# A graph layer on one core: edge groups of 2048 with per-partition sums by node, in place of groups of 1024 with one-hot products for every edge

## Chip, core and metric

The kernel runs on one core of a Trainium2 chip, in one launch. The metric is the device time of that core in microseconds (us), the median of three runs. A further execution was recorded by the hardware profiler; every duration below comes from that one recording.

## What is computed

The reference is one layer of a graph network on 6250 nodes with 64 features and 206250 edges, all fp32. The edges are sorted by their target `dst` before the kernel gets them; each node also has an edge to itself.

```python
h   = max(layernorm(x), 0)                      # 6250 x 64
msg = relu(h[src] + edge_attr)                  # 206250 x 64
agg = segment_sum(msg, dst, 6250)               # sum of the messages of each target node
out = x + relu((h + agg) @ W1 + b1) @ W2 + b2
```

A node has 33 edges on average (206250/6250), so 1024 edges in a row touch about 31 nodes and 2048 about 62.

## The kernel before, in words

**Groups.** The edges are taken in groups of `GE = P * G = 128 * 8 = 1024` in their sorted order. Partition p of group g holds the eight edges that follow each other from `g * 1024 + 8 * p`. There are `NG = 201` full groups and a tail group of four columns (`CT`), which makes `201 * 8 + 4 = 1612` columns of 128 edges.

**Loads.** For each group `load` (called from `window_sum`) gets a tile `ea` (the edge features, one 256 KB transfer on SyncE's queue, L121) and a tile `xg` (the rows `h[src]`). `xg` is filled by `gather` (L128 to L130): one indirect DMA for each column, issued by GpSimd (POOL), each with 128 row numbers that it finds in the SBUF tile `src_sb`. Both tiles come from a pool of `LOOK = 12` buffers, so that POOL and SyncE can be up to twelve groups ahead of VectorE. The first `RAW = 4` groups gather rows of the input `x` and normalise them edge by edge (`norm_edges`), since the normalised rows `h_rows` are not yet in DRAM then.

**Start.** Layer norm of all nodes (`ln_head`, `ln_rows`), the write of `h_rows`, and the transpose into `z`, a tile of 64 x 6250 that holds h (later h + agg) with features on partitions (`ln_turn`). `slot` (L219) is each edge's node number less that of the first node of its group, plus 1.

**The loop over groups, `window_sum`.** VectorE compares `slot` with the numbers 1 to 64 and gets a one-hot tile `oh` in bf16 (L294; `wslots` lies in PSUM). It adds `xg` and `ea`, both in SBUF, into `full`, a tile in PSUM (L299). ScalarE and VectorE then take turns to split relu(full) into three bf16 parts whose sum is the fp32 value (L301, L302, L304, L305). TensorE multiplies: eight products with the one-hot of a column as weights and the 192 part values as the moving operand add up in `agg`, 64 nodes x 3 x 64 (L308). One group later VectorE sums the three parts (`turn`, L278), TensorE transposes (L280), and one more group later VectorE adds the result to 64 columns of `z` that start at a register's value (`sum_into_z`, L285).

**Blocks.** When all edges of a block of 512 nodes are summed (`READY`), `hidden` and `result` do the two dense layers of it and store 128 KB through SyncE's queue (L330). The block's output tile waits for VectorE (L328), and later `ea` loads stand behind that store in the same queue.

**Order.** The order on each engine is the order of the program text: `window_sum(g)`, `turn(g-1)`, `sum_into_z(g-2)`, `blocks_behind(g-2)`. A check (`find_left`) sets a flag if an edge fell outside its window of 64 nodes or came after its block was finished; then a slow path at the end runs all edges again. It is not taken with these inputs.

Of the kernel before, what the change touches and what calls it, by code (L numbers as in the profile page):

```python
# [18 lines left out]
P = 128  # L19
G = 8  # L20
# [3 lines left out]
TP, TG = 71, 6  # L24
assert TP * TG == TE
TJ = 3
# [3 lines left out]
W = 64  # L30
WB = 512
R = 4
# [4 lines left out]
LOOK = 12  # L37
LAG = 2
RV = 8
RAW = 4  # L40
READY = [min(NG, -(-E * P * R * (c + 1) // (N * GE)) + 1) for c in range(NB)]
# [4 lines left out]
def kernel(  # L46
# [20 lines left out]
    work = ctx.enter_context(tc.tile_pool(name="work", bufs=4))  # L67
# [78 lines left out]
    def norm_edges(xg):  # L146
        s = lnp.tile([P, XC * R], F32, name="ln_s")
# [3 lines left out]
        sq = lnp.tile([P, XC * R, D], F32, name="ln_sq")  # L151
        nc.scalar.activation(sq[:, :G], xg, AF.Square)
        v = lnp.tile([P, XC * R], F32, name="ln_v")
# [6 lines left out]
    def ln_head(c):  # L160
        xv, p, n = ((x_sb[:, c:c + XC].rearrange("p b r d -> p (b r) d"), P, XC * R) if c < NB
                    else (x_sb[:TN, NB, 0:1, :], TN, 1))
        s = lnp.tile([P, XC * R], F32, name="ln_s")
# [4 lines left out]
        sq = lnp.tile([P, XC * R, D], F32, name="ln_sq")  # L168
# [3 lines left out]
    def ln_rows(c, xc, sq, p, n):  # L172
        v = lnp.tile([P, XC * R], F32, name="ln_v")
# [16 lines left out]
    def ln_turn(c, h):  # L190
        for b in range(XC if c < NB else 1):
            pt = psum.tile([D, R, P], F32, name="big", bufs=1)
            n0 = (c + b) * P * R
            if c < NB:
                for r in range(R):
                    nc.tensor.transpose(pt[:, r, :], h[:, b * R + r, :], ident)  # L196
                nc.scalar.copy(z[:, n0:n0 + P * R].rearrange("d (p r) -> d r p", r=R), pt)  # L197
            else:
                nc.tensor.transpose(pt[:, 0, :TN], h[:TN, 0, :], ident[:TN, :TN])
                nc.scalar.copy(z[:, n0:N], pt[:, 0, :TN])  # L200

    heads, rows = [], []
# [6 lines left out]
    rows.append(ln_rows(*heads[-1]))  # L209
    ln_turn(*rows[-2])  # L210
# [3 lines left out]
    base = const.tile([1, NG + 1], F32, name="base")  # L214
    nc.vector.tensor_copy(base, dst_sb[0:1, 0:C + 1:G])
    pb = psum.tile([P, R * D], F32, name="out", bufs=1)
    nc.tensor.matmul(pb[:, :NG + 1], ones[0:1, :], base, start=True, stop=True)
# [10 lines left out]

    def combine(xg, ea, n):
# [7 lines left out]
    flag = const.tile([1, 1], I32, name="flag")  # L237

    def find_left():
        nc.vector.tensor_scalar(left, slot, 1.0, None, op0=ALU.is_lt)  # L240
        nc.vector.scalar_tensor_tensor(left, slot, float(W), left, op0=ALU.is_gt, op1=ALU.add)
# [5 lines left out]
        nc.tensor.matmul(pf[0:1, 0:1], most, ones[:, 0:1], start=True, stop=True)  # L247

# [23 lines left out]

    turned = {}

    def turn(g):
        pa = aggs.pop(g)
        rows = work.tile([W, D], F32, name="agg_rows")
        nc.vector.tensor_reduce(rows, pa.rearrange("w t d -> w d t"), AX.X, ALU.add)  # L278
        pt = psum.tile([D, W], F32, name="turned", bufs=1)
        nc.tensor.transpose(pt, rows, ident[:W, :W])  # L280
        turned[g] = pt

    def sum_into_z(g):
        at = window_start(g)
        nc.vector.tensor_tensor(z[:, ds(at, W)], z[:, ds(at, W)], turned.pop(g), ALU.add)  # L285

    def window_sum(g):
        n = G if g < NG else CT
        cols = cols_of(g)
        ea, xg = loaded[g] if g < RAW else load(g)  # L290
        if g < RAW:
            norm_edges(xg)
        oh = work.tile([P, G, W], BF16, name="oh")
        nc.vector.tensor_tensor(  # L294
            oh[:, :n], slot[:, cols].unsqueeze(2).to_broadcast([P, n, W]),
            wslots.unsqueeze(1).to_broadcast([P, n, W]), ALU.is_equal)

        full = psum.tile([P, G, D], F32, name="full", bufs=2)
        nc.vector.tensor_tensor(full[:, :n], xg[:, :n], ea[:, :n], ALU.add)  # L299
        parts = work.tile([P, G, 3, D], BF16, name="parts")  # L300
        nc.scalar.activation(parts[:, :n, 0, :], full[:, :n], AF.Relu)  # L301
        nc.vector.scalar_tensor_tensor(full[:, :n], full[:, :n], 0.0, parts[:, :n, 0, :],  # L302
                                       op0=ALU.max, op1=ALU.subtract)
        nc.scalar.copy(parts[:, :n, 1, :], full[:, :n])  # L304
        nc.vector.tensor_tensor(parts[:, :n, 2, :], full[:, :n], parts[:, :n, 1, :], ALU.subtract)  # L305
        pa = psum.tile([W, 3, D], F32, name="agg", bufs=2)
        for j in range(n):
            nc.tensor.matmul(pa, oh[:, j, :], parts[:, j], start=(j == 0), stop=(j == n - 1))  # L308
# [3 lines left out]
    def hidden(c):  # L312
        n0 = c * P * R
        p, r = (P, R) if c < NB else (TN, 1)
        p1 = psum.tile([D, P * R], F32, name="big", bufs=1)
# [5 lines left out]
    def result(c, h1):  # L321
# [3 lines left out]
        for k in range(r):  # L325
            nc.tensor.matmul(p2[:p, k * D:(k + 1) * D], h1[:, k, :p], w2_sb, start=True, stop=True)  # L326
        o = work.tile([P, R, D], F32, name="o")
# [5 lines left out]
    hid = {}  # L333

    def blocks_behind(g):
        for c in sorted(hid):
            result(c, hid.pop(c))
# [4 lines left out]
    for g in range(NG + 1):  # L342
        window_sum(g)
        if g >= 1:
            turn(g - 1)
        if g >= LAG:
            sum_into_z(g - LAG)
            blocks_behind(g - LAG)
        if g == 8:
            find_left()  # L350
# [5 lines left out]
    sum_into_z(NG + 1 - LAG)  # L356
    blocks_behind(NG + 1 - LAG)
    turn(NG)
    for g in range(NG + 2 - LAG, NG + 1):
        sum_into_z(g)  # L360
        blocks_behind(g)
    hid[NB] = hidden(NB)
    for c in sorted(hid):
        result(c, hid.pop(c))


    def all_windows(msg, lf, n):
        for w in range(0, N, WB):
# [3 lines left out]
            pw = psum.tile([D, WB], F32, name="big", bufs=1)  # L372
# [7 lines left out]
    with tc.If(any_left > 0):  # L380
# [17 lines left out]
        for c in range(NB + 1):  # L398
            result(c, hidden(c))
# [39 lines left out]
```

## Time and profile before

| quantity | value |
|---|---|
| median of three runs | 2051.29 us (2049.82 to 2052.92) |
| the profiled execution's own time | 2389.6 us |
| its span, first to last instruction | 2387.8 us |
| POOL busy in the span | 1584.1 us (66%) |
| VectorE (DVE) busy | 668.4 us (28%) |
| TensorE busy (PE) | 414.4 us (17%) |
| ScalarE (ACT) busy | 267.7 us (11%) |
| mean DMA rate | 47 GB/s |
| start of the first gather, start of the last | 5.7 us, 2335.4 us |

A row of the page's list of groups names the line, the engine, the operation, what it writes and reads with shapes, the count, then busy time in us, the mean of one in ns, and after the second bar the idle time of that engine ahead of it with what ended most of it. The list of waits gives who waited for whom, the sum in us, how often, and the longest. A row of the timeline gives start and duration in us; the bracket is the idle time before it. A gather's row (DMA_INDIRECT on POOL) is the time in which POOL prepares the transfer, not that in which the rows arrive.

### The profile page before, as it was taken

What the parts mean: (1) busy time and instruction counts of PE and PEld (TensorE: products, weight loads), DVE (VectorE), ACT (ScalarE), POOL (GpSimd) and SP (SyncE); (2) the same over time, 40 slices, a digit from 0 to 9 for tenths busy, and PEclk for the clock granted to TensorE, in tenths of its full rate; (3) what the DMA queues carried; (4) which work ended last, traced back from release to release, by engine and by line L of the source; (5) the groups of instructions that cost most, each with busy time, mean ns of one, the idle gap of its engine ahead of it and who ended that gap; (6) DMA issues with size and microseconds to landing.
All of it is one profiled execution on the core that took longest, in us unless ns stands there. A gap on an engine that the chain in (4) does not pass through costs nothing.

```text
span 2387.8 us, 9645 instructions
## 1 busy us (share of the span) xinstructions
PE 414.4 (17%) x1991; PEld 287.2 (12%) x1991; DVE 668.4 (28%) x1321; ACT 267.7 (11%) x450; POOL 1584.1 (66%) x1619
## 2 busy tenths in 40 slices
PE   2000201102102202131112111111202122201123
PEld 1000201101101101020101111011201011101112
DVE  3312612213312413150213223123313123312235
ACT  3100101001100101020101101001101011101012
POOL 6775775766667666677576676575766756775751
DMA  4111112113111312211311311121311131310120
GB/s 156 39 39 31 27 26 91 26 23 89 32 22 25 94 23 48 69 28 26 92 26 22 93 30 21 49 71 20 93 31 22 27 92 22 94 35 19 26 85 8
DMA packets 87526, 112.95 MB, mean 47 GB/s; under 512 B 30949, under 2 KB 35685, under 8 KB 87461
## 3 DMA queue, kind: packets, MB, share of 16 engines
q0 software_dynamic: 51584, 52.93, 11.4%
q1 hardware_dynamic: 34628, 57.65, 7.2%
q10 hardware_dynamic: 1248, 1.70, 0.2%
q14 instruction: 49, 0.39, 0.1%
q8 instruction: 17, 0.28, 0.0%
HBM read 108.96 MB, written 3.20 MB: 47 GB/s over the span
## 4 chain that ended last, share of the span: by engine, by line
another core or an unknown queue 35%; issue 27%; POOL 16%; DVE 11%; ACT 4%; DMA 3%; DVEq 2%; PE 1%; SPq 0%; ACTq 0%; POOLq 0%
POOL xg L130 16%; DVE full L299 3%; DVE full L302 3%; DMA xg<-h_rows,src_sb 2%; ACT parts L301 2%; DVE parts L305 2%; ACT parts L304 2%; DVE oh L294 1%; DVEq L265 1%; DVE agg_rows L278 1%; DMA ea<-in_edge_attr_dram 1%; DVEq L299 1%; PE agg L308 0%; DVE z L285 0%
## 5 line engine op out<-in xcount | busy, mean ns | idle before, releaser
L130 POOL DMA_INDIRECT xg<-h_rows,src_sb x1580 | 1550.1, 981 | 738.3 <-issue 454.5
L308 PE MATMUL agg<-parts,oh 128*64 128x192 bf16 x1612 | 299.8, 367 | 935.5 <-issue 548.2
L308 PEld LDWEIGHTS <-oh 128*64 128x64 bf16 x1612 | 229.9, 168 | 989.9 <-issue 571.6
L278 DVE TENSOR_REDUCE agg_rows<-agg 64x64 f32<-64x192 f32 x202 | 69.4, 344 | 839.4 <-remote 714.3
L301 ACT ACTIVATE parts<-full 128x512 bf16<-128x512 f32 x202 | 120.2, 595 | 1610.2 <-DVE full L299 1184.5
L280 PE MATMUL turned<-ident,agg_rows 64*64 64x64 f32 x202 | 63.1, 312 | 978.7 <-issue 603.4
L302 DVE SCALAR_TENSOR_TENSOR full<-full,parts 128x512 f32<-128x512 f32 x202 | 141.1, 698 | 289.7 <-issue 135.5
L305 DVE TENSOR_TENSOR parts<-full,parts 128x512 bf16<-128x512 f32 x202 | 139.4, 690 | 131.3 <-ACT parts L304 77.9
L299 DVE TENSOR_TENSOR full<-xg,ea 128x512 f32<-128x512 f32 x202 | 138.4, 685 | 46.8 <-DMA ea<-in_edge_attr_dram 26.2
L280 PEld LDWEIGHTS turned<-ident,agg_rows 64*64 64x64 f32 x202 | 25.5, 126 | 1041.1 <-issue 651.1
L294 DVE TENSOR_TENSOR oh<-slot,wslots 128x512 bf16<-128x512 f32 x202 | 135.7, 672 | 0.0
L304 ACT CAST parts<-full 128x512 bf16<-128x512 f32 x202 | 118.0, 584 | 154.4 <-DVE full L302 110.7
L285 DVE TENSOR_TENSOR z<-z,turned 64x64 f32 x202 | 42.1, 208 | 233.7 <-issue 126.0
L130 POOL DMA_INDIRECT xg<-in_x_dram,src_sb x32 | 32.8, 1024 | 13.3 <-issue 9.4
L328 DVE TENSOR_TENSOR o<-out,x_sb 128x256 f32<-128x256 f32 (+1 forms) x13 | 5.3, 409 | 118.5 <-remote 103.7
L318 ACT ACTIVATE h<-big,b_sb 64x512 f32<-64x512 f32 (+1 forms) x13 | 8.5, 656 | 266.4 <-remote 176.8
L316 PE MATMUL big<-z,w_sb 64*64 64x512 f32 (+1 forms) x26 | 24.2, 1032 | 0.3 <-DVE z L285 0.3
L326 PE MATMUL out<-w_sb,h 64*128 64x64 f32 (+1 forms) x98 | 23.6, 418 | 1.2 <-ACT h L318 1.2
L326 PEld LDWEIGHTS out<-w_sb,h 64*128 64x128 f32 (+1 forms) x98 | 22.3, 329 | 3.2 <-ACT h L318 3.2
L196 PE MATMUL big<-ident,ln_h 128*64 128x128 f32 x48 | 12.7, 421 | 45.2 <-DVE ln_h L178 19.1
L197 ACT COPY z<-big 64x512 f32<-64x512 f32 x12 | 12.6, 1051 | 23.2 <-remote 14.4
L196 PEld LDWEIGHTS big<-ident,ln_h 128*64 128x64 f32 x48 | 6.5, 159 | 51.0 <-issue 38.9
(52 smaller groups left out, 63.7 us busy)
## 6 DMA issues: line engine op xcount, KB each, us to landing
ea<-in_edge_attr_dram SPq DMA_DIRECT2D x201, 256.0 KB
xg<-h_rows,src_sb POOLq DMA_INDIRECT x1580
x_sb<-in_x_dram SPq DMA_DIRECT2D x4, 384.0 KB
h_rows<-ln_h SPq DMA_DIRECT2D x4, 384.0 KB
out_dram<-o SPq DMA_DIRECT2D x12, 128.0 KB
dst_sb<-in_dst_main_dram ACTq DMA_DIRECT2D x1, 804.0 KB
src_sb<-in_src_main_dram ACTq DMA_DIRECT2D x1, 788.0 KB
xg<-in_x_dram,src_sb POOLq DMA_INDIRECT x32
```

The costliest lines, as they stand in the source:

```text
L130: nc.gpsimd.indirect_dma_start(out=xg[:, j, :], out_offset=None, in_=rows[:, :], in_offset=bass.IndirectOffsetOnAxis(ap=idx[:, j:j + 1], a ...
L278: nc.vector.tensor_reduce(rows, pa.rearrange("w t d -> w d t"), AX.X, ALU.add)
L280: nc.tensor.transpose(pt, rows, ident[:W, :W])
L285: nc.vector.tensor_tensor(z[:, ds(at, W)], z[:, ds(at, W)], turned.pop(g), ALU.add)
L294: nc.vector.tensor_tensor(oh[:, :n], slot[:, cols].unsqueeze(2).to_broadcast([P, n, W]), wslots.unsqueeze(1).to_broadcast([P, n, W]), ALU. ...
L299: nc.vector.tensor_tensor(full[:, :n], xg[:, :n], ea[:, :n], ALU.add)
L301: nc.scalar.activation(parts[:, :n, 0, :], full[:, :n], AF.Relu)
L302: nc.vector.scalar_tensor_tensor(full[:, :n], full[:, :n], 0.0, parts[:, :n, 0, :], op0=ALU.max, op1=ALU.subtract)
L304: nc.scalar.copy(parts[:, :n, 1, :], full[:, :n])
L305: nc.vector.tensor_tensor(parts[:, :n, 2, :], full[:, :n], parts[:, :n, 1, :], ALU.subtract)
L308: nc.tensor.matmul(pa, oh[:, j, :], parts[:, j], start=(j == 0), stop=(j == n - 1))
L326: nc.tensor.matmul(p2[:p, k * D:(k + 1) * D], h1[:, k, :p], w2_sb, start=True, stop=True)
```

## The change

- Groups have 2048 edges: `G = 16`, so each partition holds 16 edges that follow each other. There are 100 full groups and a tail of 12 columns; the number of columns is `100 * 16 + 12 = 1612`. `LOOK` is 7 groups, `RAW` is 3, `LAG` is 4, the window has 96 nodes.
- Once at the start, `cut` makes three masks over all edges on VectorE: `first` (the edge's node is that of the partition's first edge in the group), `last` (that of its last edge, unless it is the same node), and `mid` (one node between them). `run_slot` holds the three nodes' slots for each group and partition.
- In the loop the sum `xg + ea` is written back into `xg` in SBUF. For each of the three masks VectorE makes `msg = max(xg, 0) * mask` and reduces it over the partition's 16 edges into 64 values. ScalarE's splitting into bf16 parts is gone.
- TensorE gets three fp32 products for a group, with the 64 sums as weights and a one-hot of 96 columns as the moving operand. The product comes out with features on partitions, so the sum of parts, the transpose and `turn` are gone. `one_hot` runs once for two groups.
- `result` is split: the store comes at least one group later (`store`). `READY` is worked out with a margin of 1500 edges. `find_left` asks for edges that none of the three masks covers too. PSUM buffers are dealt out anew; `base` is spread earlier.

The diff, cut to its core:

```diff
-G = 8
+G = 16
+RUNS = 3
...
-W = 64
+W = 96
...
-LOOK = 12
-LAG = 2
+LOOK = 7
+LAG = 4
+OB = 2
 RV = 8
-RAW = 4
-READY = [min(NG, -(-E * P * R * (c + 1) // (N * GE)) + 1) for c in range(NB)]
+RAW = 3
+LW = max(XC * R, G)
+SPARE = 1500
+READY = [min(NG, (E * P * R * (c + 1) // N + SPARE) // GE) for c in range(NB)]
...
+    of_run = [const.tile([P, C + CT], F32, name=f"run{k}") for k in range(RUNS)]
+    run_slot = const.tile([P, NG + 1, RUNS + 1], F32, name="run_slot")
+
+    def cut(g, n, cols, k):
+
+        sv = slot[:, cols].rearrange("p (g j) -> p g j", j=k)
+        first, last, mid = [t[:, cols].rearrange("p (g j) -> p g j", j=k) for t in of_run]
+        nc.vector.tensor_tensor(first, sv, sv[:, :, 0:1].to_broadcast([P, n, k]), ALU.is_equal)
+        nc.vector.tensor_tensor(last, sv, sv[:, :, k - 1:k].to_broadcast([P, n, k]), ALU.is_equal)
+        nc.vector.tensor_tensor(last, last, first, ALU.is_gt)
+        nc.vector.tensor_copy(run_slot[:, g:g + n, 0], sv[:, :, 0])
+        nc.vector.tensor_copy(run_slot[:, g:g + n, 1], sv[:, :, k - 1])
+        nc.vector.tensor_tensor(mid, first, last, ALU.add)
+        nc.vector.scalar_tensor_tensor(mid, mid, 0.5, sv, op0=ALU.is_lt, op1=ALU.mult)
+        nc.vector.tensor_reduce(run_slot[:, g:g + n, 2], mid, AX.X, ALU.max)
+        nc.vector.tensor_tensor(mid, mid, run_slot[:, g:g + n, 2:3].to_broadcast([P, n, k]), ALU.is_equal)
+
+    cut(0, NG, slice(0, C), G)
...
+    def one_hot(g, n, runs):
+        oh = work.tile([P, OB, RUNS + 1, W], F32, name="oh", bufs=3)
+        nc.vector.tensor_tensor(
+            oh[:, :n, :runs], run_slot[:, g:g + n, :runs].unsqueeze(3).to_broadcast([P, n, runs, W]),
+            wslots.unsqueeze(1).unsqueeze(1).to_broadcast([P, n, runs, W]), ALU.is_equal)
...
     def window_sum(g):
-        n = G if g < NG else CT
-        cols = cols_of(g)
+        n, runs = (G, RUNS) if g < NG else (TJ, RUNS + 1)
+        if g % OB == 0 and g < NG:
+            one_hot(g, min(OB, NG - g), RUNS)
+        elif g == NG:
+            one_hot(g, 1, RUNS + 1)
+        oh = hots.pop(g)
         ea, xg = loaded[g] if g < RAW else load(g)
         if g < RAW:
             norm_edges(xg)
-        oh = work.tile([P, G, W], BF16, name="oh")
-        nc.vector.tensor_tensor(
-            oh[:, :n], slot[:, cols].unsqueeze(2).to_broadcast([P, n, W]),
-            wslots.unsqueeze(1).to_broadcast([P, n, W]), ALU.is_equal)
-
-        full = psum.tile([P, G, D], F32, name="full", bufs=2)
-        nc.vector.tensor_tensor(full[:, :n], xg[:, :n], ea[:, :n], ALU.add)
-        parts = work.tile([P, G, 3, D], BF16, name="parts")
-        nc.scalar.activation(parts[:, :n, 0, :], full[:, :n], AF.Relu)
-        nc.vector.scalar_tensor_tensor(full[:, :n], full[:, :n], 0.0, parts[:, :n, 0, :],
-                                       op0=ALU.max, op1=ALU.subtract)
-        nc.scalar.copy(parts[:, :n, 1, :], full[:, :n])
-        nc.vector.tensor_tensor(parts[:, :n, 2, :], full[:, :n], parts[:, :n, 1, :], ALU.subtract)
-        pa = psum.tile([W, 3, D], F32, name="agg", bufs=2)
-        for j in range(n):
-            nc.tensor.matmul(pa, oh[:, j, :], parts[:, j], start=(j == 0), stop=(j == n - 1))
+
+        sums = work.tile([P, RUNS + 1, D], F32, name="sums", bufs=LAG + 2)
+        m = n if g < NG else CT
+        nc.vector.tensor_tensor(xg[:, :m], xg[:, :m], ea[:, :m], ALU.add)
+        for k in range(RUNS):
+            msg = work.tile([P, G, D], F32, name="msg")
+            col = cols_of(g).start
+            nc.vector.scalar_tensor_tensor(
+                msg[:, :n], xg[:, :n], 0.0, of_run[k][:, col:col + n].unsqueeze(2).to_broadcast([P, n, D]),
+                op0=ALU.max, op1=ALU.mult)
+            nc.vector.tensor_reduce(sums[:, k], msg[:, :n].rearrange("p j d -> p d j"), AX.X, ALU.add)
+        if g == NG:
+            nc.vector.tensor_scalar(sums[:, RUNS], xg[:, TJ], 0.0, None, op0=ALU.max)
+        if g % OB == 0:
+            banks.append(psum.tile([D, OB, W], F32, name="agg", bufs=3))
+        pa = banks[-1][:, g % OB]
+        for k in range(runs):
+            nc.tensor.matmul(pa, sums[:, k], oh[:, k], start=(k == 0), stop=(k == runs - 1))
         aggs[g] = pa
...
     for g in range(NG + 1):
         window_sum(g)
-        if g >= 1:
-            turn(g - 1)
         if g >= LAG:
             sum_into_z(g - LAG)
             blocks_behind(g - LAG)
+        if g == 5:
+            find_left()
         if g == 8:
-            find_left()
+            judge()
```

## The prediction

> **What bounds the kernel now.** I read the page's busy times and list of groups, then the list of waits, then the timeline inside the loop, then its last microseconds. From the list of groups:
>
> ```profile
> L130 POOL DMA_INDIRECT xg<-h_rows,src_sb x1580 | 1550.1, 981 | 738.3 <-issue 454.5
> L299 DVE TENSOR_TENSOR full<-xg,ea 128x512 f32<-128x512 f32 x202 | 138.4, 685 | 46.8 <-DMA ea<-in_edge_attr_dram 26.2
> L278 DVE TENSOR_REDUCE agg_rows<-agg 64x64 f32<-64x192 f32 x202 | 69.4, 344 | 839.4 <-remote 714.3
> ```
>
> POOL's gathers are the only work near the length of the run. In a quiet stretch of the timeline a gather is busy for 0.944 us and the next follows 0.305 us later, a pitch of 1.249 us; 1612 of them make 2013 us of a span of 2387.8. The mean is 981 ns, not 944: summed over all gathers, records longer than 0.944 us add 63 us. The rest of the idle time is this, from the list of waits:
>
> ```profile
> POOL xg L130 <- DVE full L299: 262.1, 31, 16.8
> DVE agg_rows L278 <- remote: 714.3, 62, 17.5
> ```
>
> 31 times POOL was twelve groups ahead and waited for L299 to free a buffer, about 254 us beyond the usual gap. VectorE was late because it waited at L278 for TensorE, for up to 17.5 us, though TensorE's products are recorded as done long before. These waits lie 0.70 us apart (14.70, 15.39, 16.09, 16.79, 17.49), and in bursts VectorE takes a group every 4.4 us. So the profiled execution is gathers (5.7 us to the first, 2013) + lengthening 63 + waits 254 + a tail of 52 after the last gather = 2388. Without the waits, and with a tail of 18 (last gather's landing 2.2 us, then the 16 us that the last group takes from its L299 at 2371.8), it would be 2100. The median of the runs is 2051, below even that: unprofiled, POOL is not held up by TensorE at all, and its pitch, lengthening included, is at most (2051 - 6 - 18 - 2)/1612 = 1.256 us. I take the runs as bound by POOL from end to end.
>
> Where the 63 us come from is seen in the timeline of a burst:
>
> ```profile
> 1169.89 0.68 DVE L299 TENSOR_TENSOR full<-xg,ea 128x512 f32<-128x512 f32 x1
> 1170.22 1.16 POOL L130 DMA_INDIRECT xg<-h_rows,src_sb  x1 [0.30 <-issue]
> 1171.30 0.70 DVE L302 SCALAR_TENSOR_TENSOR full<-full,parts 128x512 f32<-128x512 f32 x1 [0.72 <-issue]
> 1171.69 0.94 POOL L130 DMA_INDIRECT xg<-h_rows,src_sb  x1 [0.30 <-issue]
> 1172.65 0.69 DVE L305 TENSOR_TENSOR parts<-full,parts 128x512 bf16<-128x512 f32 x1 [0.65 <-ACT parts L304]
> 1172.94 0.94 POOL L130 DMA_INDIRECT xg<-h_rows,src_sb  x1 [0.30 <-issue]
> 1174.18 1.56 POOL L130 DMA_INDIRECT xg<-h_rows,src_sb  x1 [0.30 <-issue]
> 1174.25 0.69 DVE L299 TENSOR_TENSOR full<-xg,ea 128x512 f32<-128x512 f32 x1
> ```
>
> A gather that starts during L299 is long; one that starts during L302 or L305 is not. L299 reads two SBUF tiles, L302 and L305 one of SBUF and one of PSUM. Over all gathers the rule is tight: one that starts between 0.085 us before and (duration - 0.126) us after the start of a VectorE operation with two SBUF inputs is lengthened until that operation's end less 0.126 us; others are not. L299 accounts for 52 of the 63 us. L150, L167 (tensor_tensor with a broadcast operand), L157, L178 (scalar_tensor_tensor with one) and L241 hold gathers in the same way (1.32 us at L241); the reductions L148, L154, L164, L174, L278 and L294 (one input in PSUM) do not.
>
> **What the Trainium skill says.** "SBUF — State Buffer", section "SBUF: two separate sides", says VectorE and GpSimd share a pair of SBUF ports under an exclusive lock; a VectorE operation with two SBUF inputs holds it for its whole length against a GpSimd operation that reads SBUF. The trace agrees, as above. "Vector Engine (DVE) Microarchitecture Reference", section "Measured stream behaviour on trn2", says a read keeps the full rate only while elements come in adjacent pairs, and prices a source that hops at every element at 1.73 ns a column, against 1.05. No VectorE row of this trace shows that for SBUF plainly; ScalarE's L197, which writes with a 16-byte step, takes 1051 ns for 512 columns where L301 takes 595. "Perfetto Trace Analysis", section "DMA Instruction — SWDGE (GPSIMD)", says the record ends when the descriptors are made, not at the data; here rows land 2.13 us (median) after a record of 0.944 us starts.
>
> **The change, part by part.**
> *Gathers.* 1612 before, 100 x 16 + 12 = 1612 after: nothing.
> *Removed off the path.* L301 and L304 (ACT, 238 us), L302, L305, L278 and 202 one-hots (DVE, 486 us), 1612 bf16 products and the transposes (PE): no gather waits for them in the runs, so zero. If TensorE's lag were real in the runs, see the first rival. Fp32 products, 3 a group with features out, lie in 20 us of gathers: zero.
> *VectorE's length.* L299 takes 418 ns for 256 columns and 686 for 512: 150 ns + 1.047 a column, so 1.22 us for 1024. A group then costs add 1.22 + three multiplies 3.67 + three reductions + half a one-hot 0.4 + z 0.25. A reduction reads with a step of 64 words: at full rate (L164, 947 ns for 768) 1.22 us, with the page's 1.73 ns 1.92 us (estimate). Sum 9.2 to 11.3 us, against 16 x 1.249 = 20 us of gathers. VectorE doesn't become the bound; it waits for each group's last rows.
> *The lock, in the path.* Per group of 2048 the change trades two operations with two SBUF inputs of 0.686 us for four of 1.22: the add, and three multiplies, since xg and the masks are both in SBUF. Count from the start of a group's last gather, t = 0. Rows land and the add runs 2.20 to 3.42. The gather at 2.498 is held until 3.296: 0.80. The next at 4.545 falls near the end of the first multiply (3.46 to 4.68): 0.01. One at 5.81 meets the first reduction, free. With reductions of 1.92 the second multiply is 6.57 to 7.79 (an independent operation starts some 0.075 us before the former ends, as at L353), so the gather at 7.06 is held to 7.66: 0.61. One at 8.91 is free, one at 10.16 is held 0.61 by the third multiply. Sum 2.03 us, x 100 = 203 us. Before: the add runs 2.20 to 2.886, the gather at 2.498 is held 0.26, x 201 = 52 us, which is what the profile shows. Net **+151 us**. With gathers at random phases: (1.22 - 0.04)^2/(2 x 1.249) = 0.56 for each of four, 225 us, against 0.167 x 202 = 34: +191. With the reduction as the unknown the phase alone moves the sum: at 1.30 us the second and third multiplies cost almost nothing and the net is +29; at 1.22 each gather meets a multiply at its very start and the net is +258. I take 1.92 and keep +29 and +258 as the ends. An effect below zero would need gathers to miss most of 4.9 us of lock in every 20, which the 1.249 pitch excludes.
> *Start.* `cut` and the longer `find_left` add about nine VectorE operations with two SBUF inputs over 1600 columns (1.83 us each by L219, L241), each holding a gather some 0.6 to 1.3 us: +8, range 5 to 12. With 48 raw gathers instead of 32, `h_rows` has landed when it is wanted; the one wait of 2.9 us at 50.8 goes: -2.6.
> *Queues.* Stores stay on SyncE's queue ahead of later `ea` loads, one or two groups later; loads need 512 KB per 20 us, and the next group's is first in the queue: zero. If it were late, L299's idle time now (26 us in 9 waits for `ea`) prices it, and POOL is seven groups ahead at most, so it would cost POOL nothing.
> *Tail.* Last group 12 columns: add 0.96, three multiplies 2.7, three reductions 4.1, then four products, five adds to z that stand behind it, and two blocks as now: 22 us against 18: +4.
> **Sum:** 151 + 8 - 2.6 + 4 = +160. From the profiled execution less its waits: 2100 + 160 = 2260. On the median, whose pitch is some 0.03 us shorter: 2051 + 160 = **2211 us**.
>
> **The rivals.**
> (1) *TensorE's lag is real in the runs* (ends faster). If the unprofiled pitch, lengthening included, were 1.14 us, 1612 of them are 1838, and 2025 - 1838 = 187 of the 2051 would be waits for L299; the change cuts TensorE's instructions per 2048 edges from 36 to about 12 and drops L278, and gives 2051 - 187 + 160 = 2024. It decides from 160 us of waits, a pitch below 1.157. For it: 254 us in the profile. Against it: the median is below even the sum without waits, and nothing in TensorE's own rows explains 17 us. 11%.
> (2) *Lucky phases* (reduction near 1.3, or above 2.5 us): net +29 to +75, 2090 to 2135. 22%.
> (3) *Unlucky phases* (reduction of 1.22 or 2.2 to 2.4): +205 to +258, up to 2320. 15%.
> (4) *Gathers and locks drift apart and removed holds pay for added ones:* within 0.2%. 3%.
> (5) *An edge is left by the masks and the slow path runs*: far above 4000 us; needs over three nodes in 16 edges where a node has 33. Under 1%.
>
> **Numbers.** The forecast holds 48%, at 2175 to 2235. Leaving out rival 1, rival 4 and the top of rival 3, the range is 2080 to 2290. A measurement of this kernel tells about 0.2% from no change. Faster 0.11, same 0.03, slower 0.86.
>
> **What would show it.** Gather records with a mean near 1.1 us and a lengthening above 180 us in sum, under the add and the multiplies, not under the reductions; POOL's waits for VectorE gone; the reduction's mean (1.9 expected; it sets the phase); VectorE busy near 1050 us, waiting for rows; a span of about 2260. Wrong if the gather's mean stays at 0.98, or if the time falls while the gathers' pitch doesn't.

## The result, and the profile after

The changed kernel takes **2175.87 us** (median of four runs, 2174.71 to 2176.39), the kernel before 2051.09 us beside it (four runs, 2049.82 to 2052.92): +124.8 us, a ratio of 1.0607, with an interval of 1.0588 to 1.0625. The forecast was 2211 us, its range 2080 to 2290. The profiled execution of the changed kernel takes 2176.25 us (span 2174.5), as much as its runs, so here the profile describes the runs; for the kernel before it did not (2389.6 against 2051).

One condition has to be known to read what follows. On two of the chips used below the kernel before takes 2399 and 2401 us, and a gather there comes no faster than one per 1.40 us on average, once POOL is some 19 to 26 us ahead of that rate; to judge by its time (2389.6 us) and by its waits for TensorE, the recorded execution of before shown further up is of this kind; which chip it ran on is not on record. On the chips of the comparison above and of the last two sets of experiments there is no such limit. I call the two kinds of chip limited and unlimited. Why a chip is limited is open.

From the changed kernel's list of groups; after the first bar busy us and the mean of one in ns, after the second the engine's idle time ahead and what ended it:

```profile
L134 POOL DMA_INDIRECT xg<-h_rows,src_sb x1564 | 1601.1, 1024 | 476.6 <-issue 458.7
L342 DVE TENSOR_TENSOR xg<-xg,ea 128x1024 f32<-128x1024 f32 (+1 forms) x101 | 123.5, 1223 | 936.3 <-DMA xg<-h_rows,src_sb 936.2
L349 DVE TENSOR_REDUCE sums<-msg 128x64 f32<-128x1024 f32 (+1 forms) x303 | 563.7, 1860 | 10.4
L346 DVE SCALAR_TENSOR_TENSOR msg<-xg,run 128x1024 f32<-128x1024 f32 (+1 forms) x303 | 368.0, 1214 | 3.5
```

From its list of waits (sum in us, times, longest), VectorE's and POOL's largest:

```profile
DVE xg L342 <- DMA xg<-h_rows,src_sb: 936.2, 97, 13.3
POOL xg L134 <- issue: 473.0, 1552, 0.3
```

After its first gather POOL never stands for more than its usual 0.3 us, and VectorE waits 936 us for rows: the gathers set the end, and VectorE with its 1160.5 us of work is not the bound. The mean gather of 1024 ns is 80 above an undisturbed one (0.944 us). The part of one group of 16 gathers in which VectorE works, from the timeline (start and duration in us):

```profile
1164.28 0.94 POOL L134 DMA_INDIRECT xg<-h_rows,src_sb  x1 [0.30 <-issue]
1164.48 1.23 DVE L342 TENSOR_TENSOR xg<-xg,ea 128x1024 f32<-128x1024 f32 x1 [8.00 <-DMA xg<-h_rows,src_sb]
1165.53 0.99 POOL L134 DMA_INDIRECT xg<-h_rows,src_sb  x1 [0.30 <-issue]
1165.74 1.23 DVE L346 SCALAR_TENSOR_TENSOR msg<-xg,run 128x1024 f32<-128x1024 f32 x1
1166.83 0.96 POOL L134 DMA_INDIRECT xg<-h_rows,src_sb  x1 [0.30 <-issue]
1167.00 1.87 DVE L349 TENSOR_REDUCE sums<-msg 128x64 f32<-128x1024 f32 x1
1168.09 0.94 POOL L134 DMA_INDIRECT xg<-h_rows,src_sb  x1 [0.30 <-issue]
1168.78 1.22 DVE L346 SCALAR_TENSOR_TENSOR msg<-xg,run 128x1024 f32<-128x1024 f32 x1
1169.34 1.48 POOL L134 DMA_INDIRECT xg<-h_rows,src_sb  x1 [0.30 <-issue]
1170.03 1.86 DVE L349 TENSOR_REDUCE sums<-msg 128x64 f32<-128x1024 f32 x1
1171.12 0.94 POOL L134 DMA_INDIRECT xg<-h_rows,src_sb  x1 [0.30 <-issue]
1171.81 1.21 DVE L346 SCALAR_TENSOR_TENSOR msg<-xg,run 128x1024 f32<-128x1024 f32 x1
1172.37 1.47 POOL L134 DMA_INDIRECT xg<-h_rows,src_sb  x1 [0.30 <-issue]
```

The gathers at 1169.34 and 1172.37 start 0.56 us into a multiply and are held until it has 0.13 us to go: 0.53 us each. The gather at 1168.09 starts inside a reduction (one SBUF input) and keeps its 0.94. The one at 1164.28 starts 0.20 us ahead of the add and is free; those at 1165.53 and 1166.83 start in the last fifth of the add and of the first multiply and lose 0.05 and 0.02.

Summed over all 1612 gather records of the changed kernel, what is longer than 0.944 us is 134.7 us: 106.6 under the multiplies (237 gathers), 9.7 under the add, 3.7 under the additions of `b2` to `x_sb`, and about 14.7 in the rest of the start. Gaps between gathers exceed 0.305 us by 0.1 us in all.

The same sum for the kernel before has to come from an unlimited chip. There its trace was only taken with two trims that leave L299 alone (the experiment `b_best` below): L299 holds 16 gathers for 5.9 us in sum, and 18.6 us lie after the last gather. So the +124.8 us are:

| part | after | before | difference |
|---|---|---|---|
| gathers held in the loop by the add and the multiplies | 116.3 | 5.9 | +110 |
| gathers held in the start and by `x_sb` + `b2` (before: its own recording, 62.7 in sum less 52.3 under L299) | 18.4 | 10.4 | +8 |
| tail after the last gather's start | 24.6 | 18.6 | +6 |
| start of the first gather (before: `b_nolock_again` 4.7, `b_best` 4.8), wait for `h_rows` (none in these two traces) | 4.6 | 4.7 | 0 |
| **sum** | | | **+124** |

That leaves under 1 us, which is in part luck: the 10.4 us come from the recording on a limited chip, whose first gather also starts later (5.7 us) and which waits 2.6 us for `h_rows`.

### The profile page after: what moved, and what is told of

Its sections match the earlier page's. It is cut to its first block, busy times and chain, and to the rows that moved or that the text cites. A ratio compares the mean times of both kernels' runs of the same rounds, so it can differ in the third digit from the quotient of the medians.

```text
span 2174.5 us, 5329 instructions
## 1 busy us (share of the span) xinstructions
PE 236.4 (11%) x785; PEld 120.8 (6%) x785; DVE 1160.5 (53%) x988; ACT 30.6 (1%) x44; POOL 1656.5 (76%) x1619
## 5 line engine op out<-in xcount | busy, mean ns | idle before, releaser
L134 POOL DMA_INDIRECT xg<-h_rows,src_sb x1564 | 1601.1, 1024 | 476.6 <-issue 458.7
L342 DVE TENSOR_TENSOR xg<-xg,ea 128x1024 f32<-128x1024 f32 (+1 forms) x101 | 123.5, 1223 | 936.3 <-DMA xg<-h_rows,src_sb 936.2
L349 DVE TENSOR_REDUCE sums<-msg 128x64 f32<-128x1024 f32 (+1 forms) x303 | 563.7, 1860 | 10.4
L356 PE MATMUL agg<-oh,sums 128*64 128x96 f32 x608 | 176.4, 394 | 1891.0 <-DVE sums L349 1891.0
L346 DVE SCALAR_TENSOR_TENSOR msg<-xg,run 128x1024 f32<-128x1024 f32 (+1 forms) x303 | 368.0, 1214 | 3.5
L356 PEld LDWEIGHTS agg<-oh,sums 128*64 128x64 f32 x608 | 87.8, 205 | 1993.5 <-DVE sums L349 1993.5
L134 POOL DMA_INDIRECT xg<-in_x_dram,src_sb x48 | 54.2, 1129 | 17.1 <-issue 14.3
L319 DVE TENSOR_TENSOR z<-z,agg 64x96 f32 x101 | 23.9, 236 | 33.8 <-issue 30.3
L323 DVE TENSOR_TENSOR oh<-run_slot,wslots 128x576 f32<-128x576 f32 (+1 forms) x51 | 37.4, 733 | 0.0
L158 DVE TENSOR_REDUCE ln_v<-ln_sq 128x16 f32<-128x1024 f32 x3 | 3.7, 1220 | 3.5 <-ACT ln_sq L156 3.5
## 6 DMA issues: line engine op xcount, KB each, us to landing
out_dram<-o SPq DMA_DIRECT2D x12, 128.0 KB, 1.7
```

The source lines that it names most:

```text
L134: nc.gpsimd.indirect_dma_start(out=xg[:, j, :], out_offset=None, in_=rows[:, :], in_offset=bass.IndirectOffsetOnAxis(ap=idx[:, j:j + 1], a ...
L319: nc.vector.tensor_tensor(z[:, ds(at, W)], z[:, ds(at, W)], aggs.pop(g), ALU.add)
L323: nc.vector.tensor_tensor(oh[:, :n, :runs], run_slot[:, g:g + n, :runs].unsqueeze(3).to_broadcast([P, n, runs, W]), wslots.unsqueeze(1).un ...
L342: nc.vector.tensor_tensor(xg[:, :m], xg[:, :m], ea[:, :m], ALU.add)
L346: nc.vector.scalar_tensor_tensor(msg[:, :n], xg[:, :n], 0.0, of_run[k][:, col:col + n].unsqueeze(2).to_broadcast([P, n, D]), op0=ALU.max, ...
L349: nc.vector.tensor_reduce(sums[:, k], msg[:, :n].rearrange("p j d -> p d j"), AX.X, ALU.add)
```

## Experiments

**The theory**: the lengthening of gathers by VectorE operations with two SBUF inputs accounts for nearly all of it, chiefly the second and third multiply of each group. **Rivals**: the time comes from VectorE's longer chain (the reductions, 564 us), or from TensorE's or the buffers' waits, or the phase between gathers and multiplies is not what decides.

Where a chip was limited, its totals say little of the lock, for a hold of up to 0.15 us per gather hides in a gap of 1.40 us. In those runs the beginning is still of use: until POOL is far enough ahead, gathers run 1.249 us apart. There I take the lengthening of the 16 gathers of each of the groups 12 to 18 and its median, and call it the hold per group. It is 1.09 us in the changed kernel's profile above.

### On a first limited chip (the kernel before: 2398.7 us, 2385.0 to 2411.5)

**a_psum**: the sum goes to PSUM, so that each multiply has one SBUF input; `big` goes from two buffers to one to make room.

```diff
-            pt = psum.tile([D, R, P], F32, name="big", bufs=2)
+            pt = psum.tile([D, R, P], F32, name="big", bufs=1)
...
-        nc.vector.tensor_tensor(xg[:, :m], xg[:, :m], ea[:, :m], ALU.add)
+        full = psum.tile([P, G, D], F32, name="full", bufs=1)
+        nc.vector.tensor_tensor(full[:, :m], xg[:, :m], ea[:, :m], ALU.add)
...
-                msg[:, :n], xg[:, :n], 0.0, of_run[k]...
+                msg[:, :n], full[:, :n], 0.0, of_run[k]...
```

> The changed kernel with the sum of rows and edge features written to a PSUM tile (one buffer; the blocks' PSUM tile goes from two buffers to one), so that the three multiplies read one SBUF tile and one PSUM tile. Lock theory: the multiplies hold no gather any more (107 us of the 135 us of lengthening go), only the add does: 2176 - 107 = about 2069 us, mean gather record near 0.96 us. Rival (VectorE's 53% busy time or its 11 us chain per group is the cost): the chain is as long as before, so about 2176 us.

Measured: 2271.14 us, 0.9477 of before (0.9421 to 0.9534). The hold per group falls to 0.01 us. The total is far above the expected 2069 because of the limit. Further into this kernel, POOL's timeline has:

```profile
1153.77 1.55 POOL L134 DMA_INDIRECT xg<-h_rows,src_sb  x1 [0.30 <-issue]
1155.62 1.10 POOL L134 DMA_INDIRECT xg<-h_rows,src_sb  x1 [0.30 <-issue]
1157.02 1.10 POOL L134 DMA_INDIRECT xg<-h_rows,src_sb  x1 [0.30 <-issue]
1158.42 1.09 POOL L134 DMA_INDIRECT xg<-h_rows,src_sb  x1 [0.30 <-DMA xg<-h_rows,src_sb]
1159.82 1.10 POOL L134 DMA_INDIRECT xg<-h_rows,src_sb  x1 [0.30 <-issue]
1161.22 1.09 POOL L134 DMA_INDIRECT xg<-h_rows,src_sb  x1 [0.30 <-issue]
1162.62 0.95 POOL L134 DMA_INDIRECT xg<-h_rows,src_sb  x1 [0.30 <-issue]
1163.88 0.94 POOL L134 DMA_INDIRECT xg<-h_rows,src_sb  x1 [0.30 <-issue]
```

Starts lie 1.40 us apart (1155.62, 1157.02, 1158.42, 1159.82), although VectorE runs nothing from 1156.4 to 1167.7, and then 1.25 again for a while. POOL's lead over a rate of one per 1.4005 us grows at first and then stays near 25 us here (a_pad 26, a_flat 22). That sets the total: 4.6 us to the first gather, 1611 x 1.4005 = 2256, less the lead of 25, puts the last gather at 2236 (2235.9 in the trace), and a tail of 33 follows. So the changed kernel's variants on limited chips, a_pe apart, all land at 2270 to 2278.

**a_pad**: an unused reduction of 624 columns (0.79 us, one SBUF input) ahead of the second and third multiply, to move them off the gathers.

```diff
             nc.vector.tensor_reduce(sums[:, k], msg[:, :n].rearrange("p j d -> p d j"), AX.X, ALU.add)
+            if g < NG and k < RUNS - 1:
+                pad = work.tile([P, 1], F32, name="pad")
+                nc.vector.tensor_reduce(pad, xg.rearrange("p j d -> p (j d)")[:, :PAD], AX.X, ALU.add)
```

> The changed kernel with one more VectorE reduction of 624 columns (about 0.80 us, one SBUF input, its result unused) ahead of the second and of the third multiply of each group. Lock theory with phases: the gather that now starts 0.56 us into those multiplies starts before them, and the next one just when they end, so the 0.54 us holds vanish although VectorE does 150 us more work: about 2070 us (2066 to 2090). Lock without phases (locked time alone counts): 2176 us. Rival (VectorE's length is the cost): 2176 us or more.

Measured: 2270.56 us, 0.9476 (0.9419 to 0.9532), at the limit. The hold per group is 0.04 us, with all four operations of two SBUF inputs still there. Its timeline in the stretch before the limit:

```profile
335.95 0.79 DVE L353 TENSOR_REDUCE pad<-xg 128x1 f32<-128x624 f32 x1
...
336.62 0.95 POOL L135 DMA_INDIRECT xg<-h_rows,src_sb  x1 [0.30 <-issue]
336.66 1.22 DVE L347 SCALAR_TENSOR_TENSOR msg<-xg,run 128x1024 f32<-128x1024 f32 x1
337.87 0.94 POOL L135 DMA_INDIRECT xg<-h_rows,src_sb  x1 [0.30 <-issue]
```

The gather starts 0.04 us ahead of the multiply and runs free inside it, and the next one comes as it ends. VectorE's chain is 1.6 us longer per group, and POOL loses nothing. So the hold is a matter of phase (of where the gather's start falls within VectorE's operations), and a longer chain on VectorE by itself costs POOL nothing.

**a_flat**: the reductions read 16 adjacent elements (so they sum other elements than the reference's).

```diff
-            nc.vector.tensor_reduce(sums[:, k], msg[:, :n].rearrange("p j d -> p d j"), AX.X, ALU.add)
+            flat = msg[:, :n].rearrange("p j d -> p (j d)")
+            nc.vector.tensor_reduce(sums[:, k], flat.rearrange("p (d j) -> p d j", j=n), AX.X, ALU.add)
```

> The changed kernel with the three reductions reading 16 elements that lie next to each other, in place of elements 64 words apart; the sums are then over other elements, so the sums' values are not those of the reference. Hop theory: a reduction falls from 1.86 to about 1.22 us. Lock theory with phases: then a gather starts just as the second and the third multiply begin and is held for all of them, about 1.15 us each: 2176 + 115 = about 2290 us, with VectorE 190 us less busy. Rival (VectorE's length is the cost): below 2176 us. Lock without phases: 2176 us.

Measured: 2275.84 us, 0.9498 (0.9441 to 0.9554), at the limit. The full reduction takes 1220 ns instead of 1866: the step of 64 words costs 0.63 ns a column. The hold per group is 1.03 us, not what a reduction as long as the pitch should have given. The timeline shows where that failed:

```profile
341.77 1.27 DVE L346 SCALAR_TENSOR_TENSOR msg<-xg,run 128x1024 f32<-128x1024 f32 x1
341.78 0.94 POOL L134 DMA_INDIRECT xg<-h_rows,src_sb  x1 [0.30 <-issue]
...
344.21 1.22 DVE L346 SCALAR_TENSOR_TENSOR msg<-xg,run 128x1024 f32<-128x1024 f32 x1
344.28 1.96 POOL L134 DMA_INDIRECT xg<-h_rows,src_sb  x1 [0.30 <-issue]
```

At the third multiply the gather starts 0.07 us behind it and loses 1.02 us. At the second it starts within 0.01 us of it, goes first, and the multiply is 0.05 us longer. The size of a hold was as expected; how often it falls was not.

**b_shift**: the kernel before with two unused reductions (512 and 256 columns) ahead of L299, to move that add onto a gather.

```diff
+        for cut in (G, G // 2):
+            if g < NG:
+                pad = work.tile([P, 1], F32, name="pad")
+                nc.vector.tensor_reduce(pad, xg[:, :cut].rearrange("p j d -> p (j d)"), AX.X, ALU.add)
         nc.vector.tensor_tensor(full[:, :n], xg[:, :n], ea[:, :n], ALU.add)
```

> The kernel before with two reductions of xg (512 and 256 columns, results unused) ahead of L299, which then starts about 0.94 us later after its rows have landed. Lock theory with phases: unshifted, L299 falls between two gathers' sensitive points and costs nothing in the runs; shifted, each L299 holds a gather 0.42 us: 2051 + 84 = about 2135 us (2105 to 2160). Rival (VectorE has 5 us to spare in each group, so nothing moves): 2051 us.

Measured: 2433.69 us, 1.0158 (1.0097 to 1.0219). VectorE waits 683 us for TensorE at L278, as in the recording of before, so it takes groups in bursts at no fixed phase, and gathers are held only 24 us by the add. **Inconclusive**: on this chip VectorE's waits for TensorE set the time, not the lock.

### On a second limited chip (the kernel before: 2401.0 us)

**b_nolock**: L299 as a copy of `xg` into PSUM, with one SBUF input. The edge features are left out of the sum.

```diff
-        nc.vector.tensor_tensor(full[:, :n], xg[:, :n], ea[:, :n], ALU.add)
+        nc.vector.tensor_copy(full[:, :n], xg[:, :n])
```

> The kernel before with L299 as a copy of xg into PSUM, one SBUF input; the edge features are left out of the messages. If L299 cost the runs 52 us, as the prediction took from the profiled execution: about 1999 us. If its phase makes it free in the runs (rows land and L299 starts 2.66 us after the last gather's start, past one gather and ahead of the next): 2049 to 2051 us.

Measured: 2404.98 us, 1.0006 (0.9977 to 1.0035). The lengthening falls from the 62.7 us of before's recording to 7.4 us, and the time does not move. **Inconclusive** for an unlimited chip, where the same edit is `b_nolock_again` below.

**a_lock2**: a fourth multiply, unused, at the end of each group. **a_red2**: a fourth reduction there instead.

```diff
+        if g < NG:
+            more = work.tile([P, G, D], F32, name="msg")
+            nc.vector.scalar_tensor_tensor(
+                more, xg, 0.0, of_run[0][:, col:col + n].unsqueeze(2).to_broadcast([P, n, D]),
+                op0=ALU.max, op1=ALU.mult)
```

```diff
+        if g < NG:
+            more = work.tile([P, D], F32, name="more")
+            nc.vector.tensor_reduce(more, xg.rearrange("p j d -> p d j"), AX.X, ALU.add)
```

> The changed kernel with a fourth multiply (two SBUF inputs, result unused) at the end of each group's work. Lock theory: it holds one more gather by 0.54 us: 2176 + 53 = about 2229 us. Rival (VectorE has 9 us to spare in each group, so more work at the end of it costs nothing): 2176 us.

> The changed kernel with a fourth reduction (1.86 us, one SBUF input, result unused) at the end of each group's work: the same place as the fourth multiply, half as long again. Lock theory: 2176 us, within 3. Rival (VectorE's length is the cost): some 2176 + 100 x 1.8 = 2356 us at most.

Measured: 2277.76 us, 0.9481 (0.9431 to 0.9531), and 2274.60 us, 0.9467 (0.9417 to 0.9517), both at the limit. In the stretch before it the hold per group is 1.55 us with the fourth multiply and 1.00 with the fourth reduction, against 1.09 and 1.03 in the two recordings of the changed kernel: one more two-input operation costs about 0.5 us, one more reduction, though 0.64 us longer, nothing.

**a_pe**: each group's three products are made three times, to see whether TensorE matters on such a chip (two runs).

```diff
-        for k in range(runs):
-            nc.tensor.matmul(pa, sums[:, k], oh[:, k], start=(k == 0), stop=(k == runs - 1))
+        for again in range(3):
+            for k in range(runs):
+                nc.tensor.matmul(pa, sums[:, k], oh[:, k], start=(k == 0), stop=(k == runs - 1))
```

> The changed kernel with each group's three products made three times over (each time from zero, so the sums stay), which brings TensorE's instructions per 2048 edges from 12 to 36, the number that the kernel before had. If the 254 us of waits in the profiled execution of before came from recording TensorE's instructions: the time of the runs stays at 2176 us while the profiled execution grows past it, with waits on TensorE in steps of 0.70 us. If TensorE's lag is real: runs and profile grow together. If the lag belongs to something else of before: both stay.

Measured: 2346.42 us, 0.9765 (0.9699 to 0.9832), 69 to 72 us above the two kernels beside it. From its list of waits:

```profile
PEld agg L357 <- issue: 916.1, 316, 49.8
...
POOL xg L134 <- issue: 520.2, 1557, 23.6
```

TensorE, busy for a fifth of the span, stands up to 49.8 us for nothing that the profile shows, and now POOL stands with it, up to 23.6 us. On a limited chip more work on TensorE is thus worth time. Whether it is the count of instructions is not shown: in both runs the clock granted to TensorE was 0.64 of full speed on average, against 1.00 in the recorded executions of a_lock2 and a_red2, and the two were not separated. A lower clock alone need not cost time: one run of a_red2 had 0.51 and took 2275.44 us. The kernel before has 36 instructions per 2048 edges and lies at 2400, the changed one about 12 and would lie near 2275 there (an estimate from its variants). What is limited is not settled.

### On an unlimited chip (the kernel before: 2056.86 us, 2056.13 to 2058.67)

**a_same**: the changed kernel as it is. **a_psum_again**: the edit of a_psum.

> The changed kernel as it is, beside the kernel before. On chips as in the first comparison: 2176 against 2051 us. On chips as in the experiments so far, where gathers beyond a lead of some 25 us come no faster than one per 1.40 us: 1612 x 1.40 = 2257 less a lead of 21, plus 4.6 at the start and 31 after the last gather, about 2272 us against 2399, since its own pitch of 1.325 us is below 1.40 and its holds are hidden there. If the lock sets the time on these chips too: 2176 us.

> The changed kernel with the sum in a PSUM tile, once more. On chips as in the first comparison, lock theory: 2176 - 107 = about 2069 us; rival (VectorE's chain): 2176. On chips with the 1.40 us limit: about 2271 us, and within 5 us of the changed kernel itself, whose 107 us more of lock are hidden by the limit.

Measured: a_same 2172.78 us, 1.0565 (1.0547 to 1.0583); a_psum_again **2071.88 us, 1.0066** (1.0050 to 1.0083). From the groups of a_same, and then of a_psum_again:

```profile
L134 POOL DMA_INDIRECT xg<-h_rows,src_sb x1564 | 1593.4, 1019 | 476.6 <-issue 452.3
```

```profile
L134 POOL DMA_INDIRECT xg<-h_rows,src_sb x1564 | 1497.0, 957 | 476.9 <-issue 449.1 <-DMA xg<-h_rows,src_sb 27.7
L350 DVE TENSOR_REDUCE sums<-msg 128x64 f32<-128x1024 f32 (+1 forms) x303 | 563.7, 1860 | 10.4
L347 DVE SCALAR_TENSOR_TENSOR msg<-full,run 128x1024 f32<-128x1024 f32 (+1 forms) x303 | 367.5, 1213 | 3.5
```

VectorE's reductions and multiplies take the same to 1 us (563.7 and 367.5 against the changed kernel's 563.7 and 368.0), and TensorE's work is the same. Only the side that the multiplies read from has changed. The gathers' busy time falls by 96 us, the lengthening in sum from 128.0 to 30.1 (102.9 to nothing under the multiplies), and the time by **101 us**. That settles the cause of these 101 of the 116 us by which a_same is slower than before on this chip, and it excludes VectorE's length and TensorE. What stays is 15 us above before: the start's and the first operations' holds, a tail of 24.1 us, and 8.1 us under the add.

### On another unlimited chip (the kernel before: 2052.45 us, 2049.84 to 2055.14)

**b_nolock_again**: the edit of b_nolock (the edge features left out). **b_best**: the kernel before with five raw groups, and with the additions of `b2` to `x_sb` given out one per group, since their twelve in a row hold one gather for 3.0 us.

```diff
-RAW = 4
+RAW = 5
...
-        if g == 9:
-            for c in range(NB):
-                nc.vector.tensor_tensor(x_sb[:, c], x_sb[:, c],
-                                        b2_sb.unsqueeze(1).to_broadcast([P, R, D]), ALU.add)
+        if 5 <= g < 5 + NB:
+            c = g - 5
+            nc.vector.tensor_tensor(x_sb[:, c], x_sb[:, c],
+                                    b2_sb.unsqueeze(1).to_broadcast([P, R, D]), ALU.add)
+        if g == 5 + NB:
             nc.vector.tensor_tensor(x_sb[:TN, NB, 0, :], x_sb[:TN, NB, 0, :], b2_sb[:TN], ALU.add)
```

> The kernel before with L299 as a copy of xg into PSUM (edge features left out of the messages), once more. Where the 1.40 us limit is not met: 0 to 2 us below before if L299 costs nothing for its phase; about 52 us below if the 52 us of the profiled execution were in the runs too. With the limit: as before, within 1%.

> The kernel before with the two places trimmed where its gathers still lose time at the start: five raw groups in place of four, so that h_rows has landed when it is wanted (the 2.9 us wait goes), and the twelve additions of b2 to x_sb one per group instead of back to back (the 3 us hold goes, some 0.6 us of single holds come, and 0.4 us for the fifth raw group). Lock theory: 5 us faster than before, ratio about 0.9975, where the 1.40 us limit is not met. Rival (these holds lie in slack): ratio 1.000. With the limit, where waits for VectorE set the time: no change that can be told.

Measured: b_nolock_again 2041.20 us, 0.9944 (0.9928 to 0.9959); b_best **2047.55 us, 0.9978** (0.9970 to 0.9985; 17 runs), faster than both kernels. In b_nolock_again the gain is 11 us, not the 52 that the recording of before showed under L299; and not all of it is L299's, since the holds in sum are 6.0 us there, against 16.3 worked out for before, of which L299 has 5.9, and the twelve additions of `b2` hold three gathers for 0.3 us in all instead of one for 3.0. From b_best's timeline and its waits:

```profile
1164.16 0.94 POOL L130 DMA_INDIRECT xg<-h_rows,src_sb  x1 [0.30 <-issue]
1164.24 0.70 DVE L299 TENSOR_TENSOR full<-xg,ea 128x512 f32<-128x512 f32 x1 [5.58 <-DMA xg<-h_rows,src_sb]
...
1165.41 0.94 POOL L130 DMA_INDIRECT xg<-h_rows,src_sb  x1 [0.31 <-DMA xg<-h_rows,src_sb]
```

```profile
DVE full L299 <- DMA xg<-h_rows,src_sb: 922.6, 189, 6.4
```

VectorE waits for rows in 189 of 202 groups, never for TensorE's lag. L299 begins just behind the start of one gather and ends 0.47 us ahead of the next: it fits between two starts. Which of b_best's two trims gave the 4.9 us is not separated: the holds of the start sum to 5.7 us in b_best's trace against 10.4 in before's recording, and the wait for `h_rows` is not in every execution (b_nolock_again's trace, with four raw groups, has none).

## Why the prediction was right, and where not

**What bounds the kernel: right.** Gathers from end to end. The undisturbed pitch, last gather's start less first, lengthening taken off, over 1611, is 1.248 us in the changed kernel and 1.248 in b_best. **The median's pitch "some 0.03 us shorter": right as a number, with its meaning missed.** With lengthening it is 1.288 in the recording, (2013 + 63)/1612, and 1.255 in b_best; without, it is the same. So what was shorter in the runs was the lengthening itself. The prediction's own numbers say so: its bound of 1.256 leaves 0.007 us above 1.249, or 12 us for all 1612 gathers. The 52 us under L299 could not be in the runs, and it subtracted them all the same. With 1.248 the kernel before closes by itself: 5 to the first gather, 2010 for 1611 pitches, 16 of lengthening, a tail of 19, which is a span of 2050, and a run takes 1.8 us more than its span (2176.25 against 2174.5): 2052 against the measured 2051.

**The waits of 254 us are not in the runs: right** for the runs compared, and rival 1 fell with that: on unlimited chips VectorE shows no lag behind TensorE. On limited chips the time is as long without the profiler's recording (2385 to 2420 us), so the lag is no product of it, and there the changed kernel would be the faster: 2270 to 2278 us for its variants against 2400, although none of these runs was of the changed kernel itself. So rival 1 named a real mechanism, on chips other than those of the result.

**The lock by the multiplies: right in kind, too large in sum.** Predicted +151 (203 less 52), measured +110 (116 less 6). The term that was too large comes from one number, "Rows land and the add runs 2.20 to 3.42". VectorE starts the add 2.66 us (median of the changed kernel) after the last gather's start, though the last packet of rows lands at 2.13. With 2.66, counted from the last gather as in the prediction, the gather at 2.50 is already under way and the one at 3.75 meets the last 0.1 us of the add: 9.7 us in all over 100 groups instead of 80. The second and third multiply cost 0.53 each against the predicted 0.61. So the 203 became 116. Two of the signs named beforehand were missed with it: a mean gather of 1.024 us where about 1.1 was expected, and a lengthening of 134.7 us in sum where it was to be above 180.

**The 52 us of before: wrong, by the same number; that it agreed with the profile was chance.** VectorE starts L299 2.59 us (median in b_best) after the last gather's start: just behind the gather at 2.50, and done at 3.29, ahead of the one at 3.75. In the recording shown VectorE came in bursts after waits for TensorE, and L299 held 118 gathers, not one in each of 201 groups by 0.26; 61 of them, with 38 of the 52 us, had started ahead of it. Where it only waits for rows it held 16. The two errors have opposite signs, -87 and +46 us, and with the 2.6 us for `h_rows` and 2 of the tail are the 35 by which the forecast was too high. That they partly cancel is luck.

**The reduction as what sets the phase: right, the range of its effect not shown.** 1.866 us against 1.92. "Vector Engine (DVE) Microarchitecture Reference" of the Trainium skill, section "Measured stream behaviour on trn2", gives 1.73 ns for a column of a hopping source; (1866 - 150)/1024 = 1.68 here and 1.05 with adjacent elements, so it agrees. That phase decides is shown by a_pad (0.04 us). That a reduction of 1.22 us costs +258 is not: a_flat, with 1.220, shows 1.03 us of hold per group where the unlucky rival wanted over two.

**The rule for a hold: its upper edge stands, its lower one does not carry over.** Gathers that start inside the operation are held until its end less 0.126 (the records of 1.48 and 1.96 us above). Of those that start 0 to 0.087 us ahead of it, the recording of before has 61 under L299, all held; b_best has 91, one held; a_same 61 and a_flat 157 under the add and the multiplies, none held; a_pad 90, one held. What makes the first case different stays open. With the rule's edge, gathers just ahead of L299 would have cost before some 0.6 us each; in the runs they cost nothing. "SBUF — State Buffer" of the Trainium skill, section "SBUF: two separate sides", says that whichever of the two starts first has the ports for the whole instruction and that the other fully blocks. The first half fits a_pad and b_best. The second does not: VectorE's multiply behind the gather shown in a_pad takes 1.22 us, as always, with 0.9 us of the gather still to run; in a tie (a_flat) it grew by 0.05.

**The rule's "others are not": wrong for one kind of operation.** L240 compares `slot` with a constant. It has one SBUF input and takes 0.98 us for 1612 columns, where L241 with two takes 1.84. From b_nolock_again's timeline:

```profile
111.14 0.98 DVE L240 TENSOR_SCALAR left<-slot 128x1612 f32<-128x1612 f32 x1
111.17 1.77 POOL L130 DMA_INDIRECT xg<-h_rows,src_sb  x1 [0.30 <-issue]
```

The gather is held 0.83 us, until L240's end less 0.126. In the recording that the prediction read, a gather that starts 0.45 us ahead of L240 (at 234.34) is 0.61 us too long as well; b_best has the same. L240 runs once in a kernel, so the forecast hardly moves with it. The passage of "SBUF — State Buffer" that the prediction cites for two SBUF inputs names operations in a 2-port mode beside them, which the prediction left out; whether L240 ran in such a mode, no run here shows.

**Start: right** (+8 against +8). **Tail: +6 against +4**, 24.6 us against the 22 worked out. **`h_rows`**: the changed kernel has no such gap, as said, but neither has b_nolock_again, so the -2.6 us was perhaps not there to be gained. **Removed work at zero: right**; VectorE's 492 us of added busy time also cost nothing by themselves (a_psum_again, a_red2).

## What to carry to other kernels

Where gathers issued by GpSimd are the bound, count VectorE's operations with two SBUF inputs (and those like L240), not VectorE's busy time: the change took work off two engines and cost 6%, and moving one operand to PSUM gave back 101 of 116 us on the chip where both were run. What an operation costs there depends on where it falls between two gathers, so take the delay from the gather to VectorE's start from the trace at VectorE's row (2.66 us), not at the last packet (2.13). When a profiled execution is far from the runs (2390 against 2051), a figure that hangs on when an engine arrives, such as the 52 us under L299, must not be carried over; here it was 6.

## What was not expected of the hardware

- On two chips gathers are let through at one per 1.40 us beyond a lead of 19 to 26 us, and engines stand for TensorE though its products are recorded as done; the kernel before is 17% slower there (2399 against 2051 us). That more work on TensorE lengthens the time there is shown (a_pe, some 70 us), the cause is not. Recording plays no part that shows: a_pe's recorded execution took 2345 us, its other run 2348.
- Rows are written 2.13 us after a gather's start, and VectorE moves at 2.66: half a microsecond lies between the last packet and the start of the operation that waits for it.
- The difference between nothing and the largest hold is about a tenth of a microsecond: a gather 0.04 us ahead of a multiply costs 0 (a_pad), one 0.07 us behind it 1.02 us (a_flat's third).
- Operations with two SBUF inputs directly behind each other can hold one gather through all of them: the twelve additions of `b2`, 0.41 us each, hold one for 3.7 us in the changed kernel and 3.0 in before's recording. In b_nolock and b_nolock_again three gathers get in among the same twelve, for 0.1 us each; what decides is open.
- An operation with one SBUF input can hold a gather too: L240, a comparison with a constant, for 0.83 us in b_nolock_again, while reductions (a_red2) and L299 as a copy into PSUM (b_nolock) hold none.
